# Last projection, first time-step and last norm reordered where attention hands over to Mamba

## Chip, cores and metric

One core of a Trainium2 chip runs the whole program in one launch. The metric is device time in microseconds; a smaller one is better. A "profiled execution" is one run under the hardware profiler: its span reaches from its first instruction to its last.

## What is computed (reference, cut)

A tensor of 4096 tokens by 256 channels, float32, goes through two layers. Layer 0 is a normalisation, three convolutions that give q, k and v, a channel-wise 3x3 convolution, attention over all 4096 tokens in 8 heads of 32 channels, and a 1x1 projection, added to the input. Layer 1 first adds a two-way Mamba to its input, then an expert network.

```python
x = x + conv_attention(group_norm(x))          # ..., last step: 1x1 projection (Wproj)
t = tokens(x)
t = t + mamba_block(layer_norm(t))             # layer_norm over the 256 channels
t = t + expert_ffn(layer_norm(t))

def mamba(x, ...):                             # run once forward, once on x[:, ::-1]
    xc, z = split(x @ in_proj.T)               # 512 channels each
    xc = silu(causal_conv4(xc) + conv_b)
    dt, B, C = split(xc @ x_proj.T)            # 16, 16, 16 columns
    dt = softplus(dt @ dt_proj.T + dt_b)
    h_t = exp(dt_t * A) * h_(t-1) + dt_t * B_t * xc_t      # 512 channels x 16 states
    y_t = sum_s(h_t * C_t) + xc_t * D
    return (y * silu(z)) @ out_proj.T
```

## The kernel before

Tokens are cut into 8 chunks of 512. A tile of [128, 2, 512] holds the 256 channels of one chunk. The four phases follow one another: convolutions, attention, Mamba, experts. Inside each phase the order of every engine's instructions is the order in which the code issues them (`tc.manual_schedule(engines=ORDERED)`, with TensorE, ScalarE, VectorE, GpSimd and SyncE in it). Between two phases, and for instructions outside such a block, a planner interleaves: of what it thinks ready, the instruction that stands earlier in the program goes first. The diagonal matrices `taps` and `skip` of the Mamba phase (lines L877 and L1322, on VectorE) lie outside the block.

**End of attention.** Each chunk has two groups of four heads. After the 32 key blocks of a group, `turn` multiplies the summed exponentials `s` with a matrix of ones (L1001) to get the denominators, and for the last group takes their reciprocal on VectorE (L1006); `divide` makes `oT` (L1025). `project(c, oT)` then multiplies with `wproj` (L945, two halves `co`), adds the input (L948) to `x1` and stores it to `x1d` (L950). For the last chunk (c = 7) it stops there; its norm is made in the Mamba phase. PSUM has a single-bank pool `ps1`, two three-bank buffers `ps3` (`three()`), and one bank for `av`. `aside()` takes a `ps3` buffer.

**Start of Mamba.** Sixteen steps `i` follow: chunk 0 forward, chunk 7 backward, chunk 1 forward, and so on. Each step has 32 slots. In slot `n`, VectorE runs one scan of 128x1024 elements (`recur`, L1908) and one product with C (L1913; for five slots of 32 GpSimd makes that product, `pooled`, L1918). ScalarE makes the decay `da` of slot n+1 (`decay`, L1885, into one of two PSUM buffers), GpSimd makes the inflow `dbx` of slot n+2 (`inflow`, L1895, three buffers), TensorE sums the states (L1948). Beside this, each slot takes one or more steps of a generator `prepare(i)`, which makes the input of a later step: two pairs of products (`in_pair`, L1341), the width-4 convolution as 32 matmuls (L1387) whose four results ScalarE takes over as `xc` (L1383), a silu with two table loads (L1391, L1330), and then dt, B and C. A table `LATE` gives how many steps of `prepare(1)` a slot of step 0 takes; where a slot isn't named, it is one. `prepare(1)` needs `un`, the norm of the last chunk.

Step 0 itself is prepared by a generator `start()`. Its part before the first `yield` runs ahead of slot 0: `xc` with silu (L1598), the product of `xc` with `wx` (L1607), its copy `few` (L1609), the store of B and C (L1610), then for each of four groups e `soft(e)` (a matmul L1617, L1618 and L1620 on ScalarE, L1619 on VectorE) and `rest(e)` (L1625 to L1627 on VectorE), the log (L1630), and `dt_piece` (L1461, L1472, L1474, with the stores L1476). `load_dt` (L1515) brings dt and dt times xc back, spread over the partitions; `load_bc` (L1505) does so for B and C. All these loads and stores are issued by SyncE's queue, in order. The one load on GpSimd's queue is that of `x1` from `x1d` (L1592).

The norm of the last chunk is a generator of seven steps, dealt out between these instructions by `step(norm)`: 1 the mean on TensorE (L122), 2 the subtraction on VectorE (L129), 3 the square on ScalarE (L131), 4 its mean on TensorE, 5 one row of the variance on ScalarE (L136) and two small DMAs (L138, L140), 6 the power -0.5 on GpSimd (L143) and two DMAs (L145, L146), 7 the product that gives `un` on GpSimd (L149). Then `un` is stored to `ud` (L1675). In this kernel steps 1 to 6 stand ahead of slot 0 and step 7 in slot 1.

Of the kernel before, what the change touches and what calls it, by code (L numbers as in the profile page):

```python
# [14 lines left out]
FP = mybir.dt.float32  # L15
# [4 lines left out]
ALU = mybir.AluOpType  # L20
# [4 lines left out]
P = 128  # L25
# [4 lines left out]
N = 512  # L30
NCH = NT // N
# [38 lines left out]
def drain(gen):  # L70
    while step(gen):
        pass
# [815 lines left out]
def attention_phase(cx, early, xT, wproj, qd, kd, vd, x1d, ud):  # L888
# [7 lines left out]
    nc, tc = cx.nc, cx.tc  # L896
    with ExitStack() as ctx:
        one = ctx.enter_context(tc.tile_pool(name="b_one", bufs=1))
        qp = ctx.enter_context(tc.tile_pool(name="b_q", bufs=2))
        ep = ctx.enter_context(tc.tile_pool(name="b_e", bufs=5))  # L900
        sp = ctx.enter_context(tc.tile_pool(name="b_s", bufs=2))
        sm = ctx.enter_context(tc.tile_pool(name="b_sm", bufs=1))
        wp = ctx.enter_context(tc.tile_pool(name="b_w", bufs=2))
        op = ctx.enter_context(tc.tile_pool(name="b_o", bufs=2))
        tl = ctx.enter_context(tc.tile_pool(name="b_tl", bufs=1))
        ps1 = ctx.enter_context(tc.tile_pool(name="b_ps1", bufs=1, space=PSUM))
# [13 lines left out]
        def three():  # L920
            return ps3.tile([P, 3, N], FP, name="sc", tag="sc")

        held = [False]

        def aside():

            held[0] = True
            return three()[:, 0, :]
# [7 lines left out]
        def project(c, oT):  # L936

            xr = tl.tile([P, CT, N], FP, name="xr", tag="xr")
            nc.sync.dma_start(out=xr, in_=xT[:, N * c : N * c + N].rearrange("(t p) n -> p t n", p=P))
            yield  # L940
            x1 = tl.tile([P, CT, N], FP, name="x1", tag="x1")
            for co in range(CT):
                ps = aside()
                for t in range(CT):
                    nc.tensor.matmul(  # L945
                        ps, wpj[:, t, P * co : P * co + P], oT[:, t, :], start=t == 0, stop=t == CT - 1
                    )
                nc.vector.tensor_tensor(x1[:, co, :], xr[:, co, :], ps, ALU.add)  # L948
# [12 lines left out]
            yield  # L961
# [19 lines left out]
        def weigh(g, kb, e):  # L981

            if kb == 0:
                g.av = pav.tile([P, N], FP, name="av", tag="av")
            t = g.t
            for h in range(4):
                nc.tensor.matmul(  # L987
                    g.av[32 * h : 32 * h + 32, :], vT[:, kb, P * t + 32 * h : P * t + 32 * h + 32],
                    e[:, h, :], start=kb == 0, stop=kb == NB - 1,
                )  # L990
            if kb == NB - 1:
                g.o = sm.tile([P, N], FP, name="o", tag="o")
                nc.vector.tensor_copy(g.o, g.av)  # L993

        def turn(g):


            den = three()[:, 0, :]
            for h in range(4):
                for ss in g.sums:  # L1000
                    nc.tensor.matmul(  # L1001
                        den[32 * h : 32 * h + 32, :], ones, ss[:, h, :], start=ss is g.sums[0], stop=ss is g.sums[-1]
                    )
            rs = sm.tile([P, N], FP, name="rs", tag="rs")
            if g.last:
                nc.vector.reciprocal(rs, den)  # L1006
# [25 lines left out]
        with tc.manual_schedule(engines=ORDERED):  # L1032
# [6 lines left out]
            for c in range(NCH):  # L1039
# [4 lines left out]
                for t in range(CT):  # L1044
                    g, e = Group(c, t, oT), None
                    for kb in range(NB):
                        sc = ps1.tile([P, N], FP, name="sc1", tag="sc1"), three()
# [20 lines left out]
                    turning = turn(g)  # L1068
            for block in past:
                weigh(*block)  # L1070
            drain(turning)
            for task in queue + [project(NCH - 1, oT)]:
                drain(task)

# [175 lines left out]

def mamba_phase(cx, early, w_in, w_x, w_out, w1, w2, x1d, ud, bcd, dtd, x2d, u2d, usum):

# [11 lines left out]
    with ExitStack() as ctx:  # L1268
# [63 lines left out]
        def mm_psum():  # L1332
            return pmm.tile([P, N], FP, name="mm", tag="mm")
# [253 lines left out]
        def start():  # L1587
# [14 lines left out]

                nc.vector.tensor_scalar(aneg[d], aneg[d], -1.0, -1e-30, ALU.mult, ALU.min)
            nx = DR + 2 * DS
            pd = mm_psum()
            for e in range(ET):
                nc.tensor.matmul(pd[0:nx, :], wx[0][:, e, :], xc[:, e, :], start=e == 0, stop=e == ET - 1)  # L1607
            xd = few()[0:nx, :]
# [20 lines left out]
            def log(e):  # L1629
                nc.scalar.activation(ex[:, e, :], ex[:, e, :], AF.Ln, bias=1.0)  # L1630

            soft(0)
            rest(0)
            log(0)
            for v in range(2):
                dt_piece(0, v, 0, ex, nc.vector)
            load_dt(0, 0, 0)
            load_dt(0, 0, 2)
            load_bc(0, 1)

            step(norm)
            step(norm)
            soft(1)
            step(norm)
            soft(2)
            rest(1)
            soft(3)
            step(norm)
            inflow(0)
            decay(0)  # L1650
            decay(1)
# [5 lines left out]
            for e in range(1, ET):  # L1657
                log(e)
            inflow(1)
            step(norm)  # L1660
            load_bc(0, 3)
            yield

            for h in range(2):
                z = sp.tile([P, 2, N], FP, name="z", tag="z", bufs=3)
# [6 lines left out]
                        dt_piece(0, v, 1, ex)  # L1672
                    yield
            step(norm)
            nc.sync.dma_start(out=ud[NCH - 1], in_=un)  # L1675
            drain(norm)
            yield
            dt_piece(0, 0, 2, ex)
            yield
            dt_piece(0, 1, 2)  # L1680
            yield
            for z in got["z"]:
                nc.scalar.activation(z, z, AF.Silu)
            exp_and_log()
            dt_piece(0, 0, 3, ex)
            yield
            dt_piece(0, 1, 3)
            yield

# [274 lines left out]

        AHEAD = 5

        LATE = {0: 0, 1: 0, 2: 0, 3: 0, 5: 2, 6: 2, 7: 5, 15: 2, 16: 2, 17: 2}
        LONG = {1, 9, 17, 24}

        FULL = {  # L1970
# [269 lines left out]
def kernel(  # L2240
# [5 lines left out]
    nc = tc.nc  # L2246
# [48 lines left out]
    conv_phase(cx, xT, w1, w3, w5, temp, qd, kd, vd, uk, uv)  # L2295
    with tc.tile_pool(name="early", bufs=1) as pool:
        early = Early(cx, pool, w_in, w_x, w_dt)
        attention_phase(cx, early, xT, wproj, qd, kd, vd, x1d, ud)
        mamba_phase(cx, early, w_in, w_x, w_out, w_m1, w_m2, x1d, ud, bcd, dtd, x2d, u2d, usum)
    expert_phase(cx, experts, x2d, u2d, outT)  # L2300


# [102 lines left out]
```

## Time and profile before

| what | value |
|---|---|
| median of 3 runs | 3949.72 us (3949.47 to 3956.82) |
| profiled execution, its own time | 3948.42 us |
| its span | 3946.3 us, mean granted TensorE clock 0.935 |
| busy: TensorE, VectorE, ScalarE, GpSimd | 3495.0, 3308.5, 2645.8, 1955.5 us |
| last exponential of attention (L1056) begins | 1742.64 us |
| first scan of slot 0 begins | 1787.80 us |
| scan of slot 13 begins | 1838.47 us |

The profile counts from the span's start. In the timeline, a row gives start, duration, engine, line, operation, output and inputs, shapes, and how many instructions are merged in it; in brackets stand the idle time of the engine before it and what ended that. "SPq" is the issue of a DMA by SyncE's queue; its transfer follows later.

### The profile page before, as it was taken

How to read it: one execution, taken by the hardware profiler on the slowest of the kernel's cores; microseconds unless marked ns; L12 is line 12 of the kernel's file. 1: busy time of each engine (PE TensorE's matmuls, PEld its weight loads, DVE VectorE, ACT ScalarE, POOL GpSimd, SP SyncE). 2: the span in 40 equal slices, each digit the busy share in tenths (PEclk: the TensorE clock that was granted, in tenths of full speed). 3: DMA queues.
4: the chain of work that ended last, by engine and by line, in shares of the span. 5: the costliest groups of instructions: out<-in, count | busy, mean ns of one | idle time of the engine just before them, and what ended most of it. 6: DMA issues, size and time to landing. Idle time of an engine off the chain costs nothing. (4 is left out here: it accounts for less than half of the span.)

```text
span 3946.3 us, 41780 instructions
## 1 busy us (share of the span) xinstructions
PE 3495.0 (89%) x14792; PEld 1121.7 (28%) x14792; DVE 3308.5 (84%) x2391; ACT 2645.8 (67%) x4138; POOL 1955.5 (50%) x1422
## 2 busy tenths in 40 slices
PE   6779999999999999998788888889888888876898
PEld 2334432222222222222222222223222222322444
DVE  8997678888888887778999999999999999999222
ACT  1222338988898898877777778777777777775222
POOL 3121001111111111117889899898988889887000
PEclk9989999999999999998899989989988898988999
DMA  6343246665666665563334433443434345342211
GB/s 217 112 132 104 83 143 141 128 129 112 139 120 121 137 121 118 110 146 122 127 120 124 124 126 117 118 128 118 133 119 121 104 122 152 102 130 79 65 62 57
DMA packets 184186, 471.95 MB, mean 120 GB/s; under 512 B 39205, under 2 KB 48677, under 8 KB 183710
## 3 DMA queue, kind: packets, MB, share of 16 engines
q1 hardware_dynamic: 137166, 304.26, 24.9%
q0 software_dynamic: 44496, 156.53, 19.0%
q10 hardware_dynamic: 2304, 8.39, 0.6%
q8 instruction: 118, 1.93, 0.2%
q14 instruction: 102, 0.84, 0.1%
HBM read 268.17 MB, written 79.56 MB: 88 GB/s over the span
## 5 line engine op out<-in xcount | busy, mean ns | idle before, releaser
L1895 POOL TENSOR_TENSOR dbx<-dtxr,b 128x1024 f32<-128x1024 f32 x512 | 1203.1, 2359 | 194.3 <-DVE da L1908 104.4
L1908 DVE TENSOR_TENSOR_SCAN da<-da,state,dbx 128x1024 f32<-128x1024 f32 x432 | 1014.0, 2347 | 15.7 <-ACT da L1885 7.1
L1056 ACT ACTIVATE e<-sc 128x1536 f32<-128x1536 f32 x512 | 740.2, 1446 | 1.3 <-PE sc L1050 1.3
L1885 ACT ACTIVATE da<-dtr,aneg 128x512 f32<-128x512 f32 x1024 | 708.1, 692 | 32.9 <-DMA dtr<-dtd 2.4
L977 POOL DMA_DIRECT2D s<-s x222 | 194.0, 999 | 900.6 <-DVE s L969 523.3
L969 DVE TENSOR_TENSOR s<-s,e 128x2048 f32<-128x2048 f32 x256 | 586.7, 2292 | 44.1 <-ACT e L1056 20.7
L1050 PE MATMUL sc<-q,kS 32*128 32x512 f32 x4096 | 588.3, 639 | 4.6 <-ACT e L1055 3.9
L1913 DVE TENSOR_TENSOR h<-da,c 128x1024 f32<-128x1024 f32 x432 | 529.2, 1225 | 32.5 <-DVE da L1908 0.5
L987 PE MATMUL av<-e,vT 128*32 128x512 f32 x4096 | 545.4, 605 | 2.4 <-DVE o L993 2.4
L1948 PE MATMUL y<-h,sel 128*32 128x512 f32 x2048 | 377.5, 663 | 93.1 <-DVE h L1913 68.1
L466 PE MATMUL cv<-v,u 128*128 128x512 f32 x928 | 410.3, 603 | 37.8 <-DVE pad L287 13.6
L967 DVE TENSOR_TENSOR s<-e 128x2048 f32<-128x2048 f32 x128 | 293.2, 2291 | 127.5 <-ACT e L1056 110.0
L1055 ACT ACTIVATE e<-sc 128x512 f32<-128x512 f32 x512 | 305.9, 597 | 112.8 <-PE sc L1050 58.1
L1341 PE MATMUL mm<-u,win 128*128 128x512 f32 x464 | 243.9, 667 | 69.9 <-ACT z L1449 28.9
L1050 PEld LDWEIGHTS sc<-q,kS 32*128 32x128 f32 x4096 | 163.8, 183 | 430.7 <-ACT e L1055 387.6
L1939 ACT COPY state<-da 128x2 f32<-128x2 f32 x431 | 68.7, 160 | 300.9 <-DVE h L1913 297.4
L466 PEld LDWEIGHTS cv<-v,u 128*128 128x128 f32 x928 | 178.3, 193 | 267.0 <-issue 222.3
L572 DVE SCALAR_TENSOR_TENSOR acc<-pad,wdw_s,acc 128x768 f32<-128x768 f32 (+1 forms) x182 | 224.8, 1240 | 33.3 <-ACT acc L559 27.9
L1387 PE MATMUL mm<-xp,taps 128*128 128x512 f32 x480 | 213.3, 596 | 0.6 <-DVE m L1537 0.6
L1908 DVE TENSOR_TENSOR_SCAN h<-da,state,dbx 128x1024 f32<-128x1024 f32 x80 | 187.5, 2343 | 10.3 <-ACT state L1939 9.3
L987 PEld LDWEIGHTS av<-e,vT 128*32 128x32 f32 x4096 | 80.9, 108 | 390.9 <-issue 376.7
L1918 POOL TENSOR_TENSOR h<-h,c 128x1024 f32<-128x1024 f32 x80 | 188.3, 2353 | 1.0 <-ACT state L1939 1.0
(380 smaller groups left out, 3894.1 us busy)
## 6 DMA issues: line engine op xcount, KB each, us to landing
s<-s POOLq DMA_DIRECT2D x222, 512.0 KB, 6.4
dtr<-dtd SPq DMA_DIRECT2D x128, 512.0 KB
dtxr<-dtd SPq DMA_DIRECT2D x128, 512.0 KB
b<-bcd SPq DMA_DIRECT2D x64, 256.0 KB
c<-bcd SPq DMA_DIRECT2D x64, 256.0 KB
dtd<-dt SPq DMA_DIRECT2D x64, 256.0 KB
dtd<-few SPq DMA_DIRECT2D x64, 256.0 KB
u<-uv SPq DMA_DIRECT2D x24, 640.0 KB
```

The source lines that it names most:

```text
L466: nc.tensor.matmul(rows4(ps), u[:, dy, P * ci : P * ci + P], v[:, dy : dy + HR, ci, :], start=dy + ci == 0, stop=dy == k - 1 and ci == CT - 1,
L967: nc.vector.tensor_tensor(g.part, before, e, ALU.add)
L969: nc.vector.tensor_tensor(g.part, g.part, e, ALU.add)
L987: nc.tensor.matmul(g.av[32 * h : 32 * h + 32, :], vT[:, kb, P * t + 32 * h : P * t + 32 * h + 32], e[:, h, :], start=kb == 0, stop=kb == N ...
L1050: nc.tensor.matmul(sc[1][:, h - 1, :] if h else sc[0], kS[r, t, P * kb : P * kb + P], q_t[r, t, :], start=True, stop=True,)
L1055: nc.scalar.activation(e[:, 0, :], sc[0], AF.Exp)
L1056: nc.scalar.activation(e[:, 1:4, :], sc[1], AF.Exp)
L1885: nc.scalar.activation(da[:, v, :], dts[i, e, j][0][:, v, :], AF.Exp, scale=aneg[i % 2][:, a : a + 1])
L1895: nc.gpsimd.tensor_tensor(u, dts[i, e, j][1], bcs[i, k][0][:, None, :].to_broadcast([P, 2, N]), ALU.mult)
L1908: nc.vector.tensor_tensor_scan(das[n].rearrange("p v n -> p (v n)"), da.rearrange("p v n -> p (v n)"), u.rearrange("p v n -> p (v n)"), st ...
L1913: nc.vector.tensor_tensor(h, da, bcs[i, k][1][:, None, :].to_broadcast([P, 2, N]), ALU.mult)
L1948: nc.tensor.matmul(ys[i, e][32 * j : 32 * j + 32, :], cx.sel, hs[n + j // 2][:, j % 2, :], start=False, stop=k == SQ - 1,)
```

## The change

The product of `xc` with `wx` takes the PSUM bank of the pool `ptl` (the bank that attention used for `av`), no longer one of the `mm` banks. The last group's denominators and the last chunk's projection use the single bank `ps1` (`alone()`) in place of `ps3` buffers. Two order-only dependences are added: the first matmul of the last projection comes after the matmul of `soft(0)` on TensorE, and its first addition comes after the last VectorE instruction of the first `dt_piece`s. The norm's steps move: step 1 stays ahead of slot 0, where it now follows `rest(3)`; steps 2, 3 and 4 come in slot 0, step 5 in slot 1, step 6 in slot 3, step 7 and the store of `un` in slot 5. `prepare(1)` takes no steps before slot 6, then 2, 3, 3, 3 and 2 in slots 6 to 10, so that 13 steps are done by the end of slot 10, as many as before; later slots are as before. The pool `b_w` of attention is laid out ahead of `b_sm`.

```diff
@@ attention_phase
+        def alone():
+            return ps1.tile([P, N], FP, name="sc1", tag="sc1")
-        held = [False]
+        held, behind = [False], []
@@ project(c, oT)
-                ps = aside()
+                ps = alone() if c == NCH - 1 else aside()
                 for t in range(CT):
-                    nc.tensor.matmul(
+                    ins = nc.tensor.matmul(
                         ps, wpj[:, t, P * co : P * co + P], oT[:, t, :], start=t == 0, stop=t == CT - 1
                     )
-                nc.vector.tensor_tensor(x1[:, co, :], xr[:, co, :], ps, ALU.add)
+                    if c == NCH - 1 and co + t == 0:
+                        behind.append(ins)
+                ins = nc.vector.tensor_tensor(x1[:, co, :], xr[:, co, :], ps, ALU.add)
+                if c == NCH - 1 and co == 0:
+                    behind.append(ins)
                 yield
@@ turn(g)
-            den = three()[:, 0, :]
+            den = alone() if g.last else three()[:, 0, :]
@@ end of attention_phase
+            for task in queue:
+                drain(task)
             drain(turning)
-            for task in queue + [project(NCH - 1, oT)]:
-                drain(task)
+            drain(project(NCH - 1, oT))
+    return behind
@@ start() in mamba_phase
-            pd = mm_psum()
+            pd = tl_psum()
...
+            def ahead_of(ins):
+                tc.add_manual_dep(
+                    ins.ins, next(i for i in reversed(nc.cur_bb.bb.instructions) if i.engine == ins.ins.engine).name,
+                    mybir.DependencyInfo(mybir.DependencyClass.NoSync, mybir.DependencyReason.DATA), reason="behind",
+                )
             soft(0)
+            if behind:
+                ahead_of(behind[0])
             rest(0)
             log(0)
             for v in range(2):
                 dt_piece(0, v, 0, ex, nc.vector)
+                if behind and v == 1:
+                    ahead_of(behind[1])
             load_dt(0, 0, 0)
             load_dt(0, 0, 2)
             load_bc(0, 1)
-            step(norm)
-            step(norm)
             soft(1)
-            step(norm)
             soft(2)
             rest(1)
             soft(3)
-            step(norm)
             inflow(0)
             decay(0)
             decay(1)
             rest(2)
             rest(3)
             step(norm)
             load_bc(0, 2)
             zs = in_pair(0, ET)
             for e in range(1, ET):
                 log(e)
             inflow(1)
-            step(norm)
             load_bc(0, 3)
             yield
+            step(norm, 3)
...                                   # slot 0: z copies, in_pair, two dt_pieces; slot 1: z copies
             step(norm)
-            nc.sync.dma_start(out=ud[NCH - 1], in_=un)
-            drain(norm)
             yield
             dt_piece(0, 0, 2, ex)
             yield
             dt_piece(0, 1, 2)
+            step(norm)
             yield
...                                   # slot 4: silu of z, table loads
             dt_piece(0, 0, 3, ex)
             yield
+            step(norm)
+            nc.sync.dma_start(out=ud[NCH - 1], in_=un)
+            drain(norm)
             dt_piece(0, 1, 3)
             yield
@@ mamba_phase
-        LATE = {0: 0, 1: 0, 2: 0, 3: 0, 5: 2, 6: 2, 7: 5, 15: 2, 16: 2, 17: 2}
+        LATE = {0: 0, 1: 0, 2: 0, 3: 0, 4: 0, 5: 0, 6: 2, 7: 3, 8: 3, 9: 3, 10: 2, 15: 2, 16: 2, 17: 2}
```

More of the change, by code (lines that the diff above doesn't have):

```diff
@@ L901, in attention_phase @@
         sp = ctx.enter_context(tc.tile_pool(name="b_s", bufs=2))
+        wp = ctx.enter_context(tc.tile_pool(name="b_w", bufs=2))
         sm = ctx.enter_context(tc.tile_pool(name="b_sm", bufs=1))
-        wp = ctx.enter_context(tc.tile_pool(name="b_w", bufs=2))
         op = ctx.enter_context(tc.tile_pool(name="b_o", bufs=2))
@@ L1046, in attention_phase @@
                     for kb in range(NB):
-                        sc = ps1.tile([P, N], FP, name="sc1", tag="sc1"), three()
+                        sc = alone(), three()
                         for h in range(4):
@@ L1249, in general_attention_phase, with mamba_phase @@
             drain(behind)
-def mamba_phase(cx, early, w_in, w_x, w_out, w1, w2, x1d, ud, bcd, dtd, x2d, u2d, usum):
+def mamba_phase(cx, early, w_in, w_x, w_out, w1, w2, x1d, ud, bcd, dtd, x2d, u2d, usum, behind=()):
     nc, tc = cx.nc, cx.tc
@@ L2297 @@
         early = Early(cx, pool, w_in, w_x, w_dt)
-        attention_phase(cx, early, xT, wproj, qd, kd, vd, x1d, ud)
-        mamba_phase(cx, early, w_in, w_x, w_out, w_m1, w_m2, x1d, ud, bcd, dtd, x2d, u2d, usum)
+        behind = attention_phase(cx, early, xT, wproj, qd, kd, vd, x1d, ud)
+        mamba_phase(cx, early, w_in, w_x, w_out, w_m1, w_m2, x1d, ud, bcd, dtd, x2d, u2d, usum, behind)
     expert_phase(cx, experts, x2d, u2d, outT)
```

## The prediction

> **What bounds the kernel now.** I read the page first: VectorE is at nine tenths or more from slice 19 to 37, the sixteen Mamba steps, so whatever delays or advances the scans at their start is carried to the end. Then I read the timeline of VectorE from the end of attention to slot 13 of step 0, to see when the scans start and where they wait again:
>
> ```profile
> DVE  8997678888888887778999999999999999999222
> ```
> ```profile
> 1750.88 3.36 DVE L1006 RECIPROCAL rs<-sc 128x512 f32<-128x512 f32 x1 [2.74 <-PE sc L1001]
> ...
> 1759.59 0.69 DVE L948 TENSOR_TENSOR x<-xr,sc 128x512 f32<-128x512 f32 x1 [1.47 <-PE sc L945]
> ...
> 1766.63 0.75 DVE L1619 TENSOR_SCALAR dt<-mm,small 128x512 f32<-128x512 f32 x1 [3.53 <-ACT ex L1618]
> ...
> 1781.81 2.58 DVE L1625 TENSOR_SCALAR few<-ex 128x512 f32<-128x512 f32 x1
> 1784.42 2.73 DVE L1626 SCALAR_TENSOR_TENSOR few<-few,ex 128x512 f32<-128x512 f32 x1
> 1787.19 0.69 DVE L1627 TENSOR_TENSOR dt<-dt,few 128x512 f32<-128x512 f32 x1
> 1787.80 2.35 DVE L1908 TENSOR_TENSOR_SCAN da<-da,state,dbx 128x1024 f32<-128x1024 f32 x1
> ...
> 1838.47 2.36 DVE L1908 TENSOR_TENSOR_SCAN da<-da,state,dbx 128x1024 f32<-128x1024 f32 x1 [2.96 <-ACT da L1885]
> ```
>
> The first scan starts at 1787.80. It follows `rest(3)`, whose two instructions took 2.58 and 2.73 us beside GpSimd's `dbx`, against 0.42 and 0.69 for the same lines at 1767. In slot 13 (1838.47) the scan waits 2.96 us for ScalarE. The third view is the timeline of the other engines: what released the first `dbx`, and what ScalarE did ahead of slot 13.
>
> ```profile
> 1781.73 4.87 POOL L1895 TENSOR_TENSOR dbx<-dtxr,b 128x1024 f32<-128x1024 f32 x2 [17.06 <-DMA dtxr<-dtd]
> ...
> 1796.22 2.33 POOL L149 TENSOR_TENSOR un<-ln_xc,ln_rstd 128x1024 f32<-128x1024 f32 x1
> ```
> ```profile
> 1760.43 3.60 PE L1607 MATMUL mm<-xc,wx 128*48 128x512 f32 x8 [0.87 <-DVE x L948]
> ...
> 1803.89 5.29 PE L1341 MATMUL mm<-un,win 128*128 128x512 f32 x8
> 1810.42 3.70 PE L1341 MATMUL mm<-un,win 128*128 128x512 f32 x8 [1.24 <-ACT xp L1369]
> ...
> 1823.11 7.14 PE L1387 MATMUL mm<-xp,taps 128*128 128x512 f32 x16
> ```
> ```profile
> 1830.28 0.69 ACT L1383 ACTIVATE xc<-mm,small 128x512 f32<-128x512 f32 x1 [1.15 <-PE mm L1387]
> ```
>
> From the first product with `un` (1803.89) to the last `xc` (1830.28) TensorE works almost without a gap. Behind that `xc`, ScalarE has a decay (1.42), two table loads (1.28 each), a silu (1.91) and the next decay (1.42), which end at 1838.38, and slot 13 scans at 1838.47. So this wait hangs on TensorE's run from `un`, not on VectorE.
>
> **The start, part by part.** The product L1607 stood behind the projection. Its new bank was free at 1747.7 (copy L993: 1746.99 + 0.69), `xc` was ready at 1748.85, and the denominators' matmuls end at 1750.82 (1746.53 + 4.29). It starts there, 9.6 us earlier. From its start to L1619 went 6.20 us (1760.43 to 1766.63), so TensorE and ScalarE would allow L1619 at 1757.0. On VectorE the reciprocal and `oT` end at 1754.96, and outside the hand-written order stand 15 more `taps` (1.26 + 1.26 + 0.67), 8 `skip` (2.03), b1c (0.16), then aneg (0.29), which L1619 must follow: 1754.96 + 5.67 = 1760.63. Before, aneg came after all these fillers though its input was ready at 1751, so I take L1619 at 1760.6; if the fillers give way, 1757.0. L1619 to the end of L1474 took 4.25 us (to 1770.88), so that ends at 1764.9. From there to the first `dbx` went 10.85 us, two DMA trips: 1775.7.
>
> Now the projection's store and the reload of `x1`, 0.5 MB each, move into these trips, where the DMA engines are full (last two columns: share, GB/s):
>
> ```profile
> 1780.00:1782.00 2.00, 2.00 (x4) 0.71 (x3) 1.93 (x5) 0.29 (x1) 0.27 (x1) 0.50 1.01 383
> 1782.00:1784.00 2.00, 2.00 (x5) 0.94 (x4) 2.00 (x1) 1.23 (x2) 2.00 (x1) 0.69 0.97 378
> ```
>
> At 380 GB/s 0.5 MB is 1.4 us. Between none and both (2.8) I take one: the first `dbx` at 1777.1, with ends 1772.1 (no filler, no traffic) and 1781.7 (nothing gained).
>
> The reload waits on GpSimd's own queue, ahead of every `dbx`. Additions at 1764.9 + 0.69, two matmul pairs of about 1.1 each, 0.69: `x1` ends at 1768.4. Before, its end at 1760.28 was followed by the reload's issue at 1764.12 and the first use at 1768.22, so issue is at 1772.2 (before `dbx`, so free) and use at 1776.3, with traffic 1777.7. The Trainium skill (SBUF — State Buffer, the shared port pair) says that GpSimd cannot write descriptors while VectorE runs a two-port instruction such as a float32 `tensor_scalar`, and `rest` has three of them here. By the row of the reload (issued in 0.56 us with VectorE idle) nothing is added; by the rule up to 0.42 for each, 1.3 in all, and as the two chains to `un` below lie 0.6 apart, the sum would be 0.7 us longer.
>
> The three other groups cost VectorE 3 x (0.75 + 0.42 + 0.69 + 0.69) = 7.7, with the two additions 9.0: done by about 1775 with waits, ahead of `dbx`. So the 4.2 us of slowing beside GpSimd ((2.58 - 0.42) + (2.73 - 0.69)) go, and the first scan waits for `dbx` alone: 1777.1 + 2.4 = 1779.5, **8.3 us earlier**. SyncE's queue gets the loads of B and C earlier, as no norm DMA stands between; the rows' price of those is 0.5 to 0.6 us of issue each, hidden.
>
> **The first slots.** The norm steps now sit inside them: 1.22 us of subtraction on VectorE (L129), 1.04 of square on ScalarE, and TensorE in order: mean of `x1` 1777.7 + 3.75, z pair 4.66, mean of squares 1.9 (3.78 at half clock), second z pair 3.70: 1791.7. ScalarE copies z behind it (0.58), then makes the decay of slot 3 (1.42): that scan at about 1794, before 1798.38. Half of the lead is gone here.
>
> **The second step.** `un` comes later, and this decides. GpSimd from its first `dbx`: eight `dbx` up to slot 5's issue (2.33 each, 18.6), three L1461 (3.4), two L1472 with L1474 (2.9), the power (1.24), slot 4's `pooled` product (2.36), `un` (2.33): 30.9. So `un` is ready at 1777.1 + 30.9 = 1808.0. Through `x1` it comes out alike: second z pair 1791.7, copy and row 1.2, small DMAs 2.8 (1784.75 to 1787.54), power 1.24, then 8.1 of GpSimd work ahead of the product (its DMAs, 1788.77 to at most 1796.22, took no more than 7.5), product 2.33: 1807.4. Products with `un` start at 1808.0 in place of 1803.89: **4.1 later**. The eight matmuls there already cost 5.29 against 3.70 at full clock, at a granted clock of 0.50, and TensorE stands idle ahead of them again, so I keep 5.29; the run to the last `xc` stays 26.4 (24.8 if warm). LATE puts that `xc` in slot 10 in both kernels, and the 8.19 us from it to slot 13's scan are ScalarE's own work. Slot 13 thus starts near 1842.6, **4.1 us later than before**, and the 8 us won at the start are eaten by VectorE's waits in slots 9 to 13, since ScalarE stands in order behind TensorE's convolution. From there VectorE is full again and the steps are the same.
>
> **Sum.** 3948.42 + 4.1 = 3952.5 for the profiled execution, whose time is 2.1 above its span; the median before lies 1.3 above it, so 3953.8, said as **3954**. About 0.2% (7.9 us) is what a measurement of this kernel can tell from no change; the forecast lies inside.
>
> Bank, pool and queue changes are costed at nothing: denominators in the single bank finish before their reciprocal as before; the second half of the projection must wait for the first addition (0.69, in the sum above); the pool order moves addresses whose users are over by 1768. If a tile in the moved pools did wait for the late `oT` or `x1`, the cost would be bounded by that addition's shift, 8 us on that tile.
>
> **Rivals.**
> - *The lead is kept (faster or even).* If the convolution doesn't hold ScalarE, slot 3's lead of 4.4 stays: 3949.7 - 4.4 = 3945.3; with L1619 at 1757.0 it's 3.6 more, 3941.7. Against it: four waits of `xc` L1383 on TensorE, 7.1 us together in the waits of ScalarE from slot 0 to the end of the step, already now with the convolution begun earlier.
> - *The store of `x1` falls behind the loads (slower).* SyncE is in order. If `x1`'s store is put after the four dt loads and three B/C pairs, it leaves about 1775 instead of 1768.6 (four times 0.55 to 0.6, six times 0.5 to 0.85), GpSimd's reload at 1779, `x1` is usable at 1783, and by the chain through `x1` (29.7 from use to `un`) `un` is ready at 1812.7: +8.8, 3958.5. It decides from `x1` usable after 1782.1 (+7.9). For it: readiness there is a near tie (1768.5 against 1768.6 for the loads). Against: the planner prefers the earlier instruction.
> - *The product doesn't move the first time-step.* If fillers and DMA eat it all, `dbx` starts at 1781.7, `un` is 1812.6, +8.7: 3958.4, just over the bound. The same sign, so it counts with the slower ones.
>
> **How the numbers follow.** Forecast (0 to +7.9, scans held by `un`): 0.52. Lead kept: 0.18, of which 0.10 by over 0.2%. Slower ones: 0.30. Range: below, the rival's 3945; above, 3958.5 plus 1.6 if TensorE's run is half a burst colder: 3960.1, rounded up to 3961. Faster 0.10, same 0.60, slower 0.30.
>
> **What would show it.** Right: L1607 near 1751; L1619 near 1760; `rest` without 2.6-us rows; first scan near 1779.5; `un` near 1806 to 1808; the last `xc` near 1834; slot 13 near 1842.6 with waits for ScalarE in slots 11 to 13. Wrong: no VectorE waits in slots 9 to 13 (the lead kept), or the reload L1592 after 1778, or `dbx` at 1781 or later.

## The result, and the profile after

The changed kernel took 3958.39 us (median of 22 runs, 3948.59 to 3966.09) against 3950.54 us for the kernel before (22 runs, 3943.47 to 3956.82): ratio 1.0019, 95% interval 1.0013 to 1.0025. That is slower by some 7.8 us, at the edge of the 0.2% that the prediction set as its bound for "same", and inside its range (3945 to 3961); the forecast was 3954.0. The profiled execution took 3960.56 us (before: 3948.42), its span 3958.4 us, at a granted clock of 0.938.

In this profile the last exponential of attention begins at 1747.42, before it was 1742.64. No instruction that the change moves had run by then, and kernel e1 below, which has the same instructions up to there, begins that exponential at 1741.45, so the 4.78 is scatter. Times after are therefore compared with 4.78 taken off, and below a "seam time" is counted from the start of that exponential. Lines moved by 7 to 17: the product is L1616, the first dt L1628, the scan L1925, `dbx` L1912.

The timeline of VectorE, after (the row form is that of the prediction's fences; "..." stands for rows left out):

```profile
1756.01 3.36 DVE L1013 RECIPROCAL rs<-sc 128x512 f32<-128x512 f32 x1 [3.09 <-PE sc L1008]
...
1765.15 0.74 DVE L1628 TENSOR_SCALAR dt<-mm,small 128x512 f32<-128x512 f32 x1
...
1773.90 0.69 DVE L953 TENSOR_TENSOR x<-xr,sc 128x512 f32<-128x512 f32 x1 [1.49 <-PE sc L948]
...
1778.95 0.69 DVE L1635 SCALAR_TENSOR_TENSOR few<-few,ex 128x512 f32<-128x512 f32 x1
...
1783.53 2.36 DVE L1925 TENSOR_TENSOR_SCAN da<-da,state,dbx 128x1024 f32<-128x1024 f32 x1 [3.16 <-POOL dbx L1912]
...
1801.98 2.36 DVE L1925 TENSOR_TENSOR_SCAN da<-da,state,dbx 128x1024 f32<-128x1024 f32 x1 [2.08 <-ACT state L1956]
...
1847.58 2.35 DVE L1925 TENSOR_TENSOR_SCAN h<-da,state,dbx 128x1024 f32<-128x1024 f32 x1 [5.33 <-ACT da L1902]
1853.60 2.36 DVE L1925 TENSOR_TENSOR_SCAN da<-da,state,dbx 128x1024 f32<-128x1024 f32 x1 [3.67 <-ACT da L1902]
```

The first scan, at 1783.53, is 9.05 us earlier on the common clock, and `rest` is back at 0.69 us where it had taken 2.73. But slot 3 (1801.98) is only 1.2 earlier, and slots 12 and 13 (1847.58 and 1853.60) wait 5.33 and 3.67 us for ScalarE: slot 13 begins 10.35 us later than before. The timelines of GpSimd, TensorE, ScalarE and SyncE's queue show the way there:

```profile
1778.25 0.79 POOL L1601 DMA_DIRECT2D x<-x1d  x1 [28.07 <-ACT da L1902]
1781.16 2.33 POOL L1912 TENSOR_TENSOR dbx<-dtxr,b 128x1024 f32<-128x1024 f32 x1 [2.12 <-DMA dtxr<-dtd]
1784.18 4.65 POOL L1912 TENSOR_TENSOR dbx<-dtxr,b 128x1024 f32<-128x1024 f32 x2 [0.69 <-DMA dtxr<-dtd]
...
1798.72 2.37 POOL L1912 TENSOR_TENSOR dbx<-dtxr,b 128x1024 f32<-128x1024 f32 x1 [1.39 <-DVE da L1925]
...
1812.15 2.34 POOL L1935 TENSOR_TENSOR h<-h,c 128x1024 f32<-128x1024 f32 x1 [1.87 <-ACT state L1956]
1815.41 2.35 POOL L149 TENSOR_TENSOR un<-ln_xc,ln_rstd 128x1024 f32<-128x1024 f32 x1 [0.93 <-DMA ln_rstd<-ln_inv]
```
```profile
1755.88 3.63 PE L1616 MATMUL tl<-xc,wx 128*48 128x512 f32 x8
...
1770.08 3.78 PE L948 MATMUL sc<-oT,wpj 128*128 128x512 f32 x4 [3.02 <-DVE x L953]
...
1785.70 3.75 PE L122 MATMUL tl<-x,mean_mat 128*128 128x512 f32 x4 [10.42 <-DMA b<-bcd]
...
1817.81 5.94 PE L1350 MATMUL mm<-un,win 128*128 128x512 f32 x8 [10.24 <-POOL un L149]
```
```profile
1845.40 0.69 ACT L1392 ACTIVATE xc<-mm,small 128x512 f32<-128x512 f32 x1 [4.80 <-PE mm L1396]
```
```profile
1771.53 0.53 SPq L1524 DMA_DIRECT2D dtr<-dtd  x1
1774.62 0.33 SPq L957 DMA_DIRECT2D x1d<-x  x1
1775.05 0.53 SPq L1524 DMA_DIRECT2D dtxr<-dtd  x1
```

`un` ends at 1817.76. Its first products wait for it (10.24 us idle ahead of 1817.81), the last `xc` follows 27.6 us behind, and ScalarE, in order, then has the same 8.2 us to slot 13 as before. In SyncE's queue the store of `x1` stands between the first two dt loads and holds the second by 3 us. The reload of `x1` leaves at 1778.25, behind six loads of SyncE's queue.

### The profile page after: what moved, and what is told of

Read it like the earlier page. It is cut to its first block, busy times and chain, and to the rows that moved or that the text cites. A ratio compares the mean times of both kernels' runs of the same rounds, so it can differ in the third digit from the quotient of the medians.

```text
span 3958.4 us, 41773 instructions
## 1 busy us (share of the span) xinstructions
PE 3474.6 (88%) x14792; PEld 1117.5 (28%) x14792; DVE 3304.3 (83%) x2391; ACT 2653.3 (67%) x4138; POOL 1956.2 (49%) x1422
## 5 line engine op out<-in xcount | busy, mean ns | idle before, releaser
L1912 POOL TENSOR_TENSOR dbx<-dtxr,b 128x1024 f32<-128x1024 f32 x512 | 1202.6, 2359 | 181.3 <-DVE da L1925 90.2
L1925 DVE TENSOR_TENSOR_SCAN da<-da,state,dbx 128x1024 f32<-128x1024 f32 x432 | 1014.3, 2348 | 26.8 <-ACT state L1956 9.6
L1902 ACT ACTIVATE da<-dtr,aneg 128x512 f32<-128x512 f32 x1024 | 710.1, 693 | 35.5 <-DMA dtr<-dtd 4.2
L1965 PE MATMUL y<-h,sel 128*32 128x512 f32 x2048 | 367.7, 654 | 96.1 <-DVE h L1930 70.9
L466 PE MATMUL cv<-v,u 128*128 128x512 f32 x928 | 412.6, 605 | 39.2 <-DVE pad L287 14.3
L1956 ACT COPY state<-da 128x2 f32<-128x2 f32 x431 | 69.3, 161 | 292.2 <-DVE h L1930 288.8
L1925 DVE TENSOR_TENSOR_SCAN h<-da,state,dbx 128x1024 f32<-128x1024 f32 x80 | 187.5, 2344 | 17.0 <-ACT state L1956 10.5
```

Of the source, the lines that this page charges most:

```text
L466: nc.tensor.matmul(rows4(ps), u[:, dy, P * ci : P * ci + P], v[:, dy : dy + HR, ci, :], start=dy + ci == 0, stop=dy == k - 1 and ci == CT - 1,
L1902: nc.scalar.activation(da[:, v, :], dts[i, e, j][0][:, v, :], AF.Exp, scale=aneg[i % 2][:, a : a + 1])
L1912: nc.gpsimd.tensor_tensor(u, dts[i, e, j][1], bcs[i, k][0][:, None, :].to_broadcast([P, 2, N]), ALU.mult)
L1925: nc.vector.tensor_tensor_scan(das[n].rearrange("p v n -> p (v n)"), da.rearrange("p v n -> p (v n)"), u.rearrange("p v n -> p (v n)"), st ...
L1965: nc.tensor.matmul(ys[i, e][32 * j : 32 * j + 32, :], cx.sel, hs[n + j // 2][:, j % 2, :], start=False, stop=k == SQ - 1,)
```

## Experiments

Seam times, in us, from each kernel's profile; the ratio is that of the runs to the runs of before on the same chip. Each seam time is from one profile. The change, e1 and e2 have the same instructions up to slot 5, and there their scans lie up to 1.6 us apart (60.3, 58.7, 59.9), their `un` up to 2.6; differences of that size say little.

| kernel | `un` ready | slot 0 | slot 13 | slot 31 | ratio, 95% interval |
|---|---|---|---|---|---|
| before | 55.9 | 45.2 | 95.8 | 161.5 | 1 |
| the change | 70.3 | 36.1 | 106.2 | 171.8 | 1.0019 (1.0013 to 1.0025) |
| e1 | not used | 35.8 | 101.7 | 167.3 | 1.0025 (1.0014 to 1.0036) |
| e2 | 68.9 | 35.5 | 94.8 | 165.5 | 1.0018 (1.0008 to 1.0027) |
| e3 | 72.0 | 41.3 | 108.5 | 174.2 | 1.0023 (1.0012 to 1.0033) |
| e4 | 69.3 | 56.6 | 110.3 | 175.9 | 1.0033 (1.0022 to 1.0044) |
| e5 | 67.7 | 36.8 | 102.7 | 168.3 | 1.0015 (1.0005 to 1.0024) |
| e6 | 66.2 | 32.5 | 102.1 | 167.7 | 1.0001 (0.9991 to 1.0012) |
| e7 | 55.8 | 41.6 | 96.9 | 162.5 | 0.9998 (0.9987 to 1.0008) |
| e8 | 54.6 | 39.0 | 85.6 | 155.8 | 0.9984 (0.9975 to 0.9994) |
| e9 | 53.7 | 33.3 | 82.9 | 151.1 | 0.9982 (0.9972 to 0.9991) |
| e10 | 51.4 | 33.6 | 86.1 | 153.1 | 0.9983 (0.9970 to 0.9996) |
| e11 | 57.6 | 41.6 | 92.3 | 160.2 | 0.9993 (0.9984 to 1.0003) |
| e12 | 52.9 | 33.3 | 92.1 | 162.7 | 1.0004 (0.9995 to 1.0013) |

**e1, the second step without `un`.** `prepare(1)` reads another input that has long been there, so the kernel's values are others and only its time is of use.

```diff
-            gots[1] = {"u": un}
+            gots[1] = {"u": early.u}
```

> The changed kernel, but step 1 is prepared from the input of chunk 0 (ready long before) in place of un; un is still made and stored, so only the wait for it is gone, and step 1's values are others. Measure: from the start of attention's last exponential to the scan of slot 13 and of slot 31 (before 95.8 and 161.5 us, changed 106.2 and 171.8). Theory (un comes late and holds TensorE's run of step 1): TensorE starts that run behind slot 2's sums, 10 us sooner, but its copies stay in slot 7 of ScalarE's order, so 4 to 5 us come back: 101 to 102 and 167 to 168. Rival (only the crowding of LATE holds the scans): 106 and 172. Rival (the first slots' waits are what counts): 106 and 172, and slot 8 as in the changed kernel in all three.

Measured: 101.7 and 167.3. Slot 31 is 4.5 us sooner than with the change. Of this, 1.6 us are there at slot 5, ahead of the first step of `prepare(1)`, and are scatter; so the wait for `un` is worth some 3 to 4.5 us of the change's loss. 5.9 us at slot 31 remain, so `un` is not all of it.

**e2, the second step's work spread further.**

```diff
-        LATE = {..., 5: 0, 6: 2, 7: 3, 8: 3, 9: 3, 10: 2, 15: 2, 16: 2, 17: 2}
+        LATE = {..., 5: 0, 6: 2, 7: 1, 8: 2, 9: 4, 15: 2, ..., 20: 2}
```

> The changed kernel with another LATE: 2, 1, 2, 4 steps in slots 6 to 9, one each in slots 10 to 14, two each in slots 15 to 20; the same total from slot 20 on. ScalarE's copies of the convolution come one a slot, TensorE runs ahead of them. Same measure. Theory (TensorE's run from un, with ScalarE standing in order behind it): slot 13's scan is no measure here as silu now comes later; slot 31 at 167 (about 4.5 sooner than 171.8), since each copy stands a slot later, where TensorE is done with it. Rival (un alone, however the copies are dealt): 172. Rival (LATE alone): 161 to 163.

Measured: slot 13 at 94.8, slot 31 at 165.5: 6.3 us under the change, with `un` nearly as late as there (68.9 against 70.3). The waits do not vanish, they move (from slot 13 to slot 31 it takes 70.7 us, the change 65.7), but the sum is smaller. So the bunched table, which puts ScalarE behind TensorE's convolution in slots 9 to 13, is a second part of the loss. The ratio of the whole, 1.0018, isn't told apart from the change's 1.0019; see the end of this section.

**e3 and e4, each half alone.** e3 is the kernel before with the change's norm steps and LATE. e4 is the change with the norm steps and LATE of before; its edit is the reverse one.

```diff
 (e3, on the kernel before)
-            step(norm)        # five of them ahead of slot 0
...
+            step(norm, 3)     # slot 0; then slots 1, 3 and 5
```

> The kernel before with the norm dealt over the slots and the new LATE only; the product, the banks and the projection stand as before. Same measure, and the first scan (before 45.2, changed 36.1). Theory: first dbx as before (39.1), first scan near 41.5 since the three groups now run ahead of dbx; un is ready 31 us behind the first dbx, at 70, TensorE's run starts 8.7 later than before, slot 13 at 104 to 105, slot 31 at 170. Rival (the product's place is what costs): slot 31 at 158 to 161.5, as before or sooner.

> The changed kernel with the norm's steps and LATE put back where they were: the product, first dt and their banks ahead of the last projection only. Same measure. Theory: first dt store as in the changed kernel, but the norm stands ahead of the other three groups and of slot 0, and x1 is usable some 8 to 10 us later than before, so the first scan comes at 53 to 55 (before 45.2) and slots 13 and 31 at 104 to 106 and 170 to 172: this half loses by itself too. Rival (the product ahead is a pure gain, and the dealt norm costs): first scan at 36 to 38, slot 31 at 153 to 156.

Measured: e3 slot 0 at 41.3, slot 31 at 174.2, 12.7 us behind before; e4 slot 0 at 56.6, slot 31 at 175.9, 14.5 behind. Both lose, as the theory had it, and by more: at slots 13 and 31 they are 3.5 to 4.3 us later than it said, the first scan of e4 1.6. So neither half gains alone, and at the seam each does worse than the two together. In e3 the dealt-out norm makes `un` 16 us later (72.0). In e4 the early norm steps stand in VectorE's order ahead of the other three dt groups, and with `x1` late the subtraction holds all of them. The timeline of e4's VectorE:

```profile
1787.54 1.22 DVE L129 TENSOR_TENSOR ln_xc<-x,tl 128x1024 f32<-128x1024 f32 x1 [18.08 <-PE tl L122]
1790.21 0.75 DVE L1628 TENSOR_SCALAR dt<-mm,small 128x512 f32<-128x512 f32 x1 [1.44 <-ACT ex L1627]
```

So with the projection behind the product, norm steps can't stay where they were; the question is how far they must go.

**e5, `x1` not held on VectorE.**

```diff
             for v in range(2):
                 dt_piece(0, v, 0, ex, nc.vector)
-                if behind and v == 1:
-                    ahead_of(behind[1])
```

> Times here are seam times: from the start of the last exponential of attention to the start of the scan of a slot (before: slot 0 45.2, slot 13 95.8, slot 31 161.5; after: 36.1, 106.2, 171.8). The change put two order dependences on the last chunk's projection: its matmuls come behind the first dt product on TensorE, and its addition on VectorE comes behind the work that follows the product. Here the one on VectorE is taken out, so that x1 is added as soon as its projection is there and its store stands ahead of the dt stores in SyncE's queue. Theory (un comes late because x1 comes late, and x1's store stands between the dt loads): x1 done at about 20 in place of 27.2, dtxr not held, first scan at 34 to 35.5, un ready at 63 to 66 in place of 70.3, slot 13 at 100 to 102, slot 31 at 165.5 to 168. Rival (un is late because GpSimd is full between its norm multiplications and slots 0 to 3, whenever x1 comes): un moves by under 2, slot 13 stays at 105 to 106, slot 31 at 171 to 172.

Measured: the store of `x1` leaves at 1768.95 in place of 1774.62, ahead of all dt loads, and the reload lands in 4.1 us. But the first scan is no sooner (36.8, expected 34 to 35.5), `un` comes at 67.7, only 2.7 sooner, slot 31 at 168.3, 3.5 sooner: between theory and rival. The early additions hold the first dt by 2 us, and with step 5 of the norm in slot 1, step 6 in slot 3 and step 7 in slot 5, GpSimd's order keeps `un` late: GpSimd doesn't wait for the norm's data directly ahead of `un` there, as it does in the change (0.93 us).

**e6, the fillers off VectorE.** `taps` and `skip` of the first direction are made on GpSimd.

```diff
-            diagonals(cx, tp, d)
+            nc.gpsimd.tensor_tensor(tp, <identity, broadcast>, <convw, broadcast>, ALU.mult)
...
-                nc.vector.tensor_scalar(skip[d]..., <identity>, <dp>, None, ALU.mult)
+                nc.gpsimd.tensor_tensor(skip[d]..., <identity>, <dp, broadcast>, ALU.mult)
```

> Seam times as in the run before. The change as it is, but the diagonal filters and skip diagonals of the first direction that VectorE makes between the last exponential and the first dt are made on GpSimd, which is idle there. Theory (VectorE's queue of small work ahead of the first dt holds it by 3 to 4 us): first dt 2 to 3.6 sooner, first scan at 32.5 to 34.5 in place of 36.1, slot 31 at 168 to 170. Rival (the first scan waits for loads, or the lead is eaten by the wait for un in any case): first scan sooner by under 1, or sooner and slot 13 still at 105.5 to 106.5, slot 31 at 171 to 172.

Measured: slot 0 at 32.5, slot 13 at 102.1, slot 31 at 167.7, close to what the theory had (4.1 us for 3.6 at the start, `un` 4.1 sooner with it).

**e7, only the dt groups earlier, on the kernel before.**

```diff
-            step(norm); step(norm); soft(1); step(norm); soft(2); rest(1); soft(3); step(norm)
-            inflow(0); decay(0); decay(1); rest(2); rest(3); step(norm)
+            soft(1); soft(2); step(norm); rest(1); soft(3); step(norm, 2); rest(2); rest(3)
+            step(norm); inflow(0); decay(0); decay(1); step(norm)
```

> Seam times as in the runs before. The kernel before, not the change: only the order in its preparation of the first chunk is other: the dt groups 1 to 3 are taken ahead of the norm steps that stood between them, and rest 2 and 3 ahead of slot 0 in place of beside its first GpSimd products. Theory (the first scan waits for a VectorE stream that holds norm steps that nobody waits for yet): first scan at 41 to 42.5 in place of 45.2, slot 13 at 92 to 93.5, slot 31 at 157.5 to 159.5, the whole 2 to 4 us under before. Rival (the norm that is later by this makes un late, as in the change): first scan the same, but slot 13 at 95.5 to 99 and slot 31 at 161 to 164.5, no gain.

Measured: slot 0 at 41.6 as expected by both, but slot 13 at 96.9 and slot 31 at 162.5. The rival's numbers came out: 3.6 us won on the first scan are worth nothing here. Its reason did not: `un` is ready when it was before (55.8 against 55.9), and TensorE takes it up 2.2 us sooner (59.1 against 61.3). GpSimd, VectorE and ScalarE of e7 show where the lead went:

```profile
1782.46 4.72 POOL L1894 TENSOR_TENSOR dbx<-dtxr,b 128x1024 f32<-128x1024 f32 x2 [16.87 <-DMA dtxr<-dtd]
...
1796.77 2.34 POOL L149 TENSOR_TENSOR un<-ln_xc,ln_rstd 128x1024 f32<-128x1024 f32 x1
```
```profile
1784.84 2.36 DVE L1907 TENSOR_TENSOR_SCAN da<-da,state,dbx 128x1024 f32<-128x1024 f32 x1 [4.56 <-POOL dbx L1894]
...
1796.84 2.36 DVE L1907 TENSOR_TENSOR_SCAN da<-da,state,dbx 128x1024 f32<-128x1024 f32 x1 [1.33 <-POOL dbx L1894]
...
1804.80 2.36 DVE L1907 TENSOR_TENSOR_SCAN da<-da,state,dbx 128x1024 f32<-128x1024 f32 x1 [1.01 <-POOL dbx L1894]
...
1840.14 2.36 DVE L1907 TENSOR_TENSOR_SCAN da<-da,state,dbx 128x1024 f32<-128x1024 f32 x1 [2.96 <-ACT da L1884]
```
```profile
1809.66 0.20 ACT L1367 COPY xp<-halos 128x12 f32<-128x12 f32 x1 [1.42 <-POOL dt L1461]
```

The edit moves work on VectorE, but GpSimd's first `dbx` is no sooner than before (39.2 against 39.1). The scans run up to GpSimd's order, wait for `dbx` in slots 3 to 5 (1.33, 0.99, 1.01), and at slot 5 the lead is gone (61.5 against 61.6). Then ScalarE's copy `xp` waits 1.42 us for GpSimd's `dt`, where it had no wait before, the last `xc` comes 1.1 later (88.7 against 87.6), and slot 13 again waits 2.96 us for ScalarE. So it was GpSimd's order that took the lead, not `un`.

**e8 to e10, the norm early within the changed order.** e8 is the change with e5's and e6's edits and five norm steps ahead of slot 0, the sixth in slot 1, the seventh with the store of `un` in slot 3; LATE starts at slot 5 and is spread as in e2. With such a table the last `xc` comes within 2.2 us of slot 13's scan (8.2 ahead of it in the change), so from here on slot 31 is the measure.

```diff
             soft(3)
+            step(norm)
             inflow(0); decay(0)
-            decay(1); rest(2); rest(3); step(norm)
+            rest(2); step(norm); rest(3); step(norm); decay(1)
...
+            step(norm)                      # 4th, 5th ahead of the first yield; 6th in slot 1
             dt_piece(0, 1, 2)
             step(norm)                      # 7th, slot 3
```

> Seam times as in the runs before. The change with VectorE's order dependence out and the diagonals made on GpSimd, and the norm put back early: its first five steps ahead of slot 0, the sixth in slot 1, the seventh and the store of un in slot 3, and decay 1 behind them; the second step's fillers begin at slot 5. Theory (the change wins its lead on the first scan and loses it, and more, on un): first scan at 31 to 35, un ready at 53 to 58 in place of 70.3, slot 13 at 88 to 93, slot 31 at 153 to 159, so 3 to 8 us under before at slot 31. Rival (what delays TensorE's run on un is not un but TensorE's and ScalarE's own queue in slots 5 to 13): un sooner as said, slot 13 at 97 to 104 and slot 31 at 163 to 170.

Measured: `un` at 54.6, slot 13 at 85.6 (better than expected), slot 31 at 155.8, 5.7 under before; the whole run is faster, 0.9984. But the first scan came at 39.0, not 31 to 35. The timelines of e8's GpSimd and VectorE show why:

```profile
1776.30 7.60 POOL L1915 TENSOR_TENSOR dbx<-dtxr,b 128x1024 f32<-128x1024 f32 x3 [7.39 <-DMA dtxr<-dtd]
```
```profile
1776.35 1.22 DVE L129 TENSOR_TENSOR ln_xc<-x,tl 128x1024 f32<-128x1024 f32 x1 [5.41 <-PE tl L122]
1777.49 1.44 DVE L1637 TENSOR_SCALAR few<-ex 128x512 f32<-128x512 f32 x1
1778.96 2.73 DVE L1638 SCALAR_TENSOR_TENSOR few<-few,ex 128x512 f32<-128x512 f32 x1
1781.73 2.72 DVE L1639 TENSOR_TENSOR dt<-dt,few 128x512 f32<-128x512 f32 x1
1784.37 2.35 DVE L1928 TENSOR_TENSOR_SCAN da<-da,state,dbx 128x1024 f32<-128x1024 f32 x1
```

The first `dbx` was done at about 1778.6, and the scan stood behind `rest`, slowed beside GpSimd, while VectorE had been idle for 5.41 us just before. e9 moves `rest(2)` and `rest(3)` into that idle time.

```diff
             step(norm)
+            rest(2); rest(3)
             inflow(0); decay(0)
-            rest(2)
             step(norm)
-            rest(3)
             step(norm); decay(1)
```

> Seam times as in the runs before (before: slot 0 45.2, slot 13 95.8, slot 31 161.5; e8: 39.0, 85.6, 155.8, un at 54.5). e8 with one thing moved: the sums of dt groups 2 and 3 on VectorE (rest 2 and 3), which in e8 stand behind the norm's subtraction and then run beside GpSimd's first products at 2.7 us in place of 0.7, are put ahead of that subtraction, into the 5.4 us in which VectorE waits for it. Theory (in e8 the first scan is held by these sums: dbx was there at 33.2, the scan began at 39.0): first scan at 33 to 35, slot 13 at 80 to 84, slot 31 at 150 to 154. Rival (as in e7, where the first scan came 3.6 sooner and slot 31 not at all: the end is set by the run on un): first scan at 33 to 35, but slot 13 at 84.5 to 87, slot 31 at 154.5 to 157.

Measured: slot 0 at 33.3, slot 13 at 82.9, slot 31 at 151.1: the theory's numbers, 10.4 us under before, and the earliest slot 31 of all. The whole run took 3942.30 us (median of 10), 0.9982 of before (0.9972 to 0.9991), against 1.0019 for the change. Of the 11.9 us won at the start 10.4 are kept at slot 31. `un` is only 2.2 us sooner than before (53.7 against 55.9), but GpSimd's first `dbx` is 8.2 sooner (30.9 against 39.1), other than in e7:

```profile
1775.60 7.09 POOL L1915 TENSOR_TENSOR dbx<-dtxr,b 128x1024 f32<-128x1024 f32 x3 [7.46 <-DMA dtxr<-dtd]
```

The LATE table is also another than in before and e7, and no run gives e7 this table; e10 and e11 below, which share one, show that the gain isn't the table's alone.

e10 puts the squares' mean ahead of the z products, the power in slot 0 and the product to `un` in slot 2, with the `dt_piece`s of group 1 one slot later and LATE from slot 4.

> Seam times as above. e9 with the norm still earlier: the matmuls of the squares ahead of the z tiles' matmuls on TensorE, the power in slot 0 ahead of GpSimd's dt pieces, the multiplication that makes un in slot 2 in place of 3; the dt pieces one slot later each, and the second step's fillers from slot 4. Theory (un's time sets the end of the first step): un at 46 to 50 in place of 54.5, slot 31 at 147 to 152. Rival (with un this early the end of the first step is set by ScalarE's queue of the second step's work): un as said, slot 31 within 2 of e9's.

Measured: `un` at 51.4, short of 46 to 50; slot 31 at 153.1, 2.0 behind e9: outside the theory's range and at the rival's edge. The scans of slots 2 and 5 wait there 2.00 and 2.69 us for ScalarE, where e9's don't wait (e9's slot 6 waits 2.44 for `dbx`; the expectation of e12 calls it slot 5). An earlier `un` brought nothing more here; the whole runs of e9 and e10 (0.9982 and 0.9983) aren't told apart.

**e11, e10 without the product half.** The projection stays ahead of the product, as before.

> Seam times as above. The kernel before with everything of e10 but the product half of the change: the last chunk's projection stays ahead of the first dt product, as before. It asks what the product's place is worth once the norm is early. Theory (the place of the product is worth its lead on the first scan): first scan 5 to 9 later than e10's (39 to 43), slot 31 4 to 9 later than e10's. Rival (it is worth nothing, since un, which comes sooner with the projection first, sets the end): un at 44 to 50, first scan later as said, slot 31 within 2 of e10's or under it.

Measured: slot 0 8.0 later than e10's (41.6), slot 31 7.1 later (160.2), with the same LATE table: what the product's place wins on the first scan it keeps almost in full, once the norm doesn't take it back. The whole runs agree in direction (medians 3947.16 and 3943.07 us on one chip), but their intervals overlap. `un` was expected at 44 to 50 and came at 57.6, although `x1` was there sooner: step 7 stands in GpSimd's queue behind the `dbx` of the first slots, and these began 8 us later.

**e12, dt pieces later.** e9 with the pieces of groups 2 and 3 in slots 5, 6, 7 and 9.

```diff
-            dt_piece(0, 0, 2, ex); yield; dt_piece(0, 1, 2)          # slots 2, 3
-            dt_piece(0, 0, 3, ex); yield; dt_piece(0, 1, 3)          # slots 4, 5
+            dt_piece(0, 0, 2, ex); yield; dt_piece(0, 1, 2); yield   # slots 5, 6
+            dt_piece(0, 0, 3, ex); yield; yield; dt_piece(0, 1, 3)   # slots 7, 9
```

> Seam times as in the runs before (e9: slot 0 33.3, slot 3 43.9, slot 8 65.5, slot 13 82.9, slot 31 151.1). e9 with the dt pieces of groups 2 and 3 on GpSimd dealt later: from slots 2, 3, 4 and 5 to slots 5, 6, 7 and 9. Theory (in e9 the scans of slots 5 and 8 wait 2.4 and 2.2 for dbx, since GpSimd has the pieces, un and nine products of dbx within nine slots; with the pieces later these waits go): slot 8 at 61 to 64, slot 13 at 79 to 82, slot 31 at 147.5 to 150.5. Rival (what is won there is lost again to the run on un and to ScalarE's queue in slots 9 to 20): slot 8 as said, slot 31 within 1 of e9's.

Measured: slot 8 at 70.8, slot 31 at 162.7: wrong on both accounts. ScalarE and VectorE of e12:

```profile
1813.40 0.20 ACT L1379 COPY xp<-halos 128x12 f32<-128x12 f32 x1 [11.20 <-POOL dt L1473]
```
```profile
1816.19 2.36 DVE L1932 TENSOR_TENSOR_SCAN da<-da,state,dbx 128x1024 f32<-128x1024 f32 x1 [8.15 <-ACT da L1909]
```

The second step's `xp` takes the buffer of the first step's `ex`, and the last reader of `ex` is `dt_piece(0, 0, 3)` on GpSimd. Moved later, it held ScalarE by 11.2 us, and the scans behind it by 8.15. (In e10 the same copy waited 2.01.)

**Seam and whole run.** The seam says 10.4 us for the change, the medians 7.8. Taken as a share of the whole, the difference to before at slot 31 lies inside the measured interval in eleven of the twelve experiments; in e6 (1.0016 by the seam, at most 1.0012 measured) and in the change (1.0026, at most 1.0025) it lies above. From slot 32 to the end the fourteen profiles take 2031.9 to 2044.0 us, and the last exponential begins at 1741.5 to 1747.4, in no order that goes with an edit, so the whole of a single profile says little below some 12 us. The later steps go with the clock: from slot 32 to the last scan the profile of e9, at a granted clock of 0.941, takes 1736.2 us, that of e1, at 0.932, 1747.3, and over the fourteen profiles the correlation of this time with the clock is -0.93. Whether the clock makes the time or the waits make the clock, no run shows.

## Why the prediction was right or wrong

In kind the account held: the start is won, `un` comes later, and the wait behind TensorE's run eats the lead and more. In size it did not: slot 13 was put 4.1 us later and came 10.35 later. Of its signs, `un` (1813.0 for 1806 to 1808), the last `xc` (1840.6 for 1834) and slot 13 (1848.8 for 1842.6) are 5 to 7 us late. That the medians, 7.8 us apart, still lie within the 7.9 us called even is luck: the seam's loss would by itself have been over it. The terms, by the clock of before:

- **The start.** L1607 at 1751.1 (1750.8 predicted), L1619 at 1760.4 (1760.6, with the fillers ahead of it, which e6 confirmed), the end of the first pieces at 1764.6 (1764.9), first `dbx` at 1776.4 (1777.1), first scan 9.05 us earlier (8.3), no slow `rest`. All within 0.8 us.
- **`x1`.** Done at 1769.8 (1768.4), usable at 1780.9 (1777.7). The second half of the projection, behind TensorE's wait for the addition, ran at a granted clock of 0.50 and took 3.78 us, where about 2.2 were allowed, and the reload took 7.2 us to land in place of 4.0. Slot 3 was at 1797.2 (about 1794).
- **`un`, the term that failed.** The prediction let GpSimd run without a gap from the first `dbx` to `un`: 30.9 us. The work took 30.8, but 5.7 us of waiting lay in between: for dtxr held by `x1`'s store (0.69), for scans and the states after them (1.39, 0.18, 1.87), and for the norm's small DMAs (0.61, 0.93). So `un` was ready at 1813.0, not 1808.0. The chain through `x1` was put at 29.7 us from use to `un` and took 32.1; the two accounts, thought 0.6 apart, were both short.
- **TensorE's run** from `un` to the last `xc` took 27.6 us (26.4), and from there to slot 13's scan 8.20 (8.19). Its first eight matmuls took 5.94 us at a granted clock of 0.62, not 5.29; the 5.29 of before were at 0.50 in their first half only, 0.70 over all. Sum at slot 13: 4.1 + 5.0 + 1.2 = 10.3 later, measured 10.35.

"The lead is kept" is excluded: slots 12 and 13 wait 5.33 and 3.67 us. The second rival's size came out (`un` at 1812.7, 3958.5 us), but not by its point: the reload was usable at 1780.9, below 1782.1, and the store passed all but the first load. The forecast mechanism with 5 us more of GpSimd's idle time gives the same number. "The product doesn't move the first time-step" is excluded by the first scan.

One thing the prediction did not look at: it kept the LATE table as neutral ("in slot 10 in both kernels"). e1 and e2 show that part of the loss hangs on that table and not on `un` alone: at slot 31 another table took 6.3 of the 10.4 us away, the wait for `un` at most 4.5. How much is each one's share can't be separated from these runs, since they overlap.

On the rule of the Trainium skill (SBUF — State Buffer, section "SBUF: two separate sides") that GpSimd can't write descriptors while VectorE holds the ports they share: the reload was issued in 0.79 us with `rest` around it, against 0.56 with VectorE idle. So 0.2 us at most, where the rule's reading allowed up to 1.3; but only one of the three `tensor_scalar` (0.42 us, at 1778.50) fell into the issue, so this is no test of the rule. The larger part of the delay, 3.2 us, was in the landing.

## What to carry to other kernels

A lead on one engine is worth what the in-order engines that feed it pass on: e7 won 3.6 us on VectorE's first scan and kept nothing, since GpSimd's first product was no sooner; e9 won 11.9 and kept 10.4, with GpSimd 8.2 sooner and `un` not later. When a step is dealt out over a loop, price its place in each in-order queue with the waits of that queue, not with its work alone (30.8 us of work took 36.6), and look at who shares its buffers (e12). Work that slows beside a neighbour belongs in the idle time ahead of it: two `rest`s moved by some lines brought 5.7 us at the first scan and 4.7 at slot 31 (e8 to e9).

## What was unexpected of the hardware

- The reload of `x1`, 0.5 MB on GpSimd's queue, took 3.9 to 4.2 us to land in the nine kernels where it was issued ahead of the first dt load on SyncE's queue, and 6.9 to 7.8 us in the four where it was issued 6.1 to 6.7 us behind it (the change, e1, e2, e6). In e4, 12.5 us behind, it took 4.6. The issue itself was 0.56 to 0.79 us. Being ahead of the other loads by 0.4 us (e8 to e10, e12) was enough.
- TensorE's granted clock halved though it had worked a third of the time: after the change it was 1.00 from 1764.33 to 1767.74, with TensorE busy for 1.12 of these 3.41 us, and 0.50 from there on, 0.7 us into a wait of 3.02. The four matmuls at the end of that wait (L948) took 3.78 us at 0.50; in e8 the same four, which follow the matmuls before without a wait, took 1.98 us at 1.00.
- `rest`'s instructions, 0.69 us alone, took 2.73 us (L1638) and, the plain `TENSOR_TENSOR` L1639, 2.72 beside `dbx` in e8; in the kernel before, L1626 took 2.73 beside `dbx` and L1627, beside no `dbx`, 0.69; the scan and the product with C kept their 2.35 and 1.23 us beside GpSimd's work.
